# Last layer of a two-layer graph kernel: aggregate the packed binary features first, multiply by the signed weight afterwards

## The chip, the cores and the metric

The kernel runs on one core of a Trainium2 chip. The metric is the device time of one execution in microseconds, as the median of several runs. An execution has five engines that run their own instruction queues in order: PE (TensorE, matmuls and its weight loads), DVE (VectorE), ACT (ScalarE), POOL (GpSimd) and SP (SyncE, which here only starts DMAs). POOL also starts DMAs from its own queue. Engines wait for one another by semaphores.

## The reference, cut to what matters

There are N = 3327 nodes and D = 512 features. `adj` is a 3327 x 3327 matrix of zeros and ones, about 1% of them ones.

```python
# two attention layers (L0), then
x = layernorm(x + L0(x, adj, W_stack))
# the last layer:
bw  = sign(weight)                    # 512 x 512, values -1, 0, 1
ba  = max(sign(x), 0)                 # 3327 x 512, values 0, 1
out = relu(adj @ (ba @ bw.T))
x   = layernorm(x + out)
```

An attention layer is `proj = x @ W`, split into `Wh` and `Ws`, `a = softmax(Wh Ws^T) * adj`, `leaky_relu(a @ Wh + x)`.

## The kernel before, in words

Rows are cut into NT = 26 tiles of 128 (the last has 127). Two tiles make a half-chunk `g`, and NQ = 13 half-chunks of 256 columns cover the matrix. For each of the two attention layers `l` there is `project(l)`, which makes keys and values with a Strassen-like scheme of seven products in place of eight, and `attention(l)`, which walks over 169 steps `(g, q)`: query half-chunk `g` against key half-chunk `q`.

The order of all work is written out by hand. In step `v` of `attention`, a list `work` of pairs (place in the step between 0 and 1, closure) is sorted and issued; each engine's queue is then in that order. PE gets seven f32 products of step `v` for the aggregation (`values`, L834) and the scores of a step 30 half-steps ahead (`scores`, L588). DVE subtracts the column maximum (`shift`), adds the running total, multiplies by the adjacency (`masked`, L769) and ACT takes the exponential. POOL then makes four sums of that block (`sums`, L807 to L810), which PE reads two steps later.

Preparation of the last layer is strewn into the same steps:

- For half of the steps of each layer, the adjacency block of the step (`adj`, 128 x 512 f32, four buffers, loaded by SP) is turned into a Strassen set of seven fp8 blocks: `halved_sums` makes four sums on DVE (L789), `halved` copies the other three on ACT (L775, L776), `keep_blocks` stores the 112 KB to memory from POOL's queue (L792). `exact` (DVE, L798) counts entries that are neither 0 nor 1.
- When a half-chunk `g` of layer 1 is done, `finish(g)` returns a list of closures, one popped per step: `residual`, `sign` (moments of the row and the binary feature `ba`), `lay` and `turn` (store to memory, reload in another layout, transpose), `linear` (`ba @ bw`, four PE matmuls with 512 columns, L953), and a store of `xw`.
- `load_products` reloads `xw` and makes its Strassen sums on DVE (`product_sums`, L212 to L215).

After the last step comes a `fill`: PE runs products of the last layer while DVE ends `finish(12)`. Then `finale` runs over the 13 half-chunks. In half-chunk `g`, PE does 7 x 13 = 91 aggregation matmuls (`aggregate`, L1199: fp8 adjacency as the stationary operand, f16 features of 256 columns as the moving one). `take_out` combines the seven products on ACT and DVE. Per tile, `standard` (two ACT operations) normalizes `h`, `moments` (three DVE operations, then an ACT square root) adds the aggregate and takes mean and variance, and `scaled` (DVE reciprocal and scaling, then a store from POOL's queue) writes the output tile. `load_h(g + 1)` is issued by SP in the middle of half-chunk `g`; the tiles `ho` have four buffers, so the load of tile t waits until the store of tile t - 4 has landed. The places of the steps of the half-chunk before are

```python
(0.05, lambda: take_out(g - 1, 3)),
(0.12 if g == NQ - 1 else 0.08, lambda: scaled(u1, nc.gpsimd)),
(0.1, lambda: moments(u2, c_of[g - 1][1])),
(0.2, lambda: scaled(u2, nc.gpsimd)),
```

The last half-chunk is followed by a branch on the count of `exact`; the slow branch is not taken with these inputs.

Of the kernel before, what the change touches and what calls it, by code (L numbers as in the profile page):

```python
# [9 lines left out]
F32 = mybir.dt.float32  # L10
# [16 lines left out]
FAR = -1e30  # L27


@with_exitstack  # L30
def kernel(
# [51 lines left out]
    ident_h = keep.tile([P, P], BF16, name="ident_h")  # L83
    nc.vector.tensor_copy(ident_h, ident)
# [7 lines left out]

# [10 lines left out]
    ba_d = tc.dram_tile([NT, P, D], BF16, name="ba_d")  # L103
    xw_d = tc.dram_tile([NT, P, D], F16, name="xw_d")
    adj_d = tc.dram_tile([NQ, P, NQ, 7, P], F8, name="adj_d")
# [443 lines left out]
    def binary_weight(k, wt):  # L549
        neg = ring.tile([P, D], BF16, tag="xr", name=f"neg_w_{k}")  # L550
        nc.vector.tensor_scalar(neg, wt, 0.0, None, ALU.is_lt)
        sg = keep.tile([P, D], BF16, name=f"bw_{k}")
        nc.vector.scalar_tensor_tensor(sg, wt, 0.0, neg, ALU.is_gt, ALU.subtract)
        bw.append(sg)

    def attention(l, att):
# [215 lines left out]
        def halved(g, q):  # L772

            at, t = adj[g, q], adj[g, q, "b"]
            nc.scalar.copy(t[:, 0:2], at[:, :, :P], saturate=False)  # L775
            nc.scalar.copy(t[:, 2], at[:, 1, P:], saturate=False)  # L776

        def halved_sums(g, q):
            at = adj[g, q]
            t = adj[g, q, "b"] = att.tile(  # L780
                [P, 7, P], F8, tag="adj_b", bufs=3, name=f"ab_{l}_{g}_{q}"
            )
            a11, a21, a12, a22 = (at[:, k, ts(i, P)] for k in range(2) for i in range(2))
            s1, s2, s3, s4 = (t[:, i] for i in range(3, 7))
            for to, a, b, op in (
                (s1, a21, a22, ALU.add), (s2, s1, a11, ALU.subtract),
                (s3, a11, a21, ALU.subtract), (s4, a12, s2, ALU.subtract),
            ):
                nc.vector.tensor_tensor(to, a, b, op, saturate=False)  # L789
# [4 lines left out]
        def exact(g, q):  # L794

            at = adj.pop((g, q))
            i = g * NQ + q
            nc.vector.scalar_tensor_tensor(  # L798
                at, at, 0.0, at, ALU.is_gt, ALU.not_equal, accum_out=cnt[:, i : i + 1],
            )  # L800
# [72 lines left out]
        def finish(g):  # L873
# [37 lines left out]
            def sign(i):  # L911

                t, hh = mine[i], hs[i]
                r = rows(t)
                st = small.tile([P, 6], F32, tag="bn", name=f"bn_{t}")
                nc.vector.bn_stats(st[:r], hh[:r])
                nc.vector.bn_aggr(mv[:r, t, :], st[:r])
                ba = held[i] = att.tile([P, D], BF16, tag="ba", bufs=1, name=f"ba_{t}")
                nc.vector.tensor_scalar(ba[:r], hh[:r], mv[:r, t, 0:1], None, ALU.is_gt)
                if g < NQ - 2:  # L920
                    nc.gpsimd.dma_start(out=ba_d[t], in_=ba)

            def lay(i):

                bt = held[i] = ring.tile([P, P // B, P], BF16, tag="xr", name=f"bt_{mine[i]}")
                load_laid(nc.sync, bt, ba_d[mine[i]], P)

            def turn(i):

                r = rows(mine[i])  # L930
                if g < NQ - 2:
                    bt = held[i]
                    held[i] = att.tile([P, KD, P], BF16, tag="baT", bufs=1,
                                       name=f"baT_{mine[i]}")
                    nc.vector.transpose(
                        held[i].rearrange("p k (r v) -> p r k v", v=B),
                        bt.rearrange("p r (u k) -> p r k u", u=B),
                    )
                    return
                by_tile = held[i].rearrange("p (u k) -> p k u", k=KD)  # L940
                pt = ps_tr.tile([P, KD, P], BF16, tag="tr", name=f"pbt_{mine[i]}")
                for k in range(KD):
                    nc.tensor.transpose(pt[:, k, :r], by_tile[:r, k], ident_h[:r, :r])
                held[i] = att.tile([P, KD, P], BF16, tag="baT", bufs=1, name=f"baT_{mine[i]}")
                nc.scalar.copy(held[i][:, :, :r], pt[:, :, :r])

            def linear(i):

                t = mine[i]
                r = rows(t)  # L950
                pw = ps_tr.tile([P, D], F32, tag="tr", name=f"pxw_{t}")
                for k in range(KD):
                    nc.tensor.matmul(  # L953
                        pw[:r], held[i][:, k, :r], bw[k], start=(k == 0), stop=(k == KD - 1)
                    )
                if g >= NQ - 2:
                    nc.scalar.copy(xw[t][:r], pw[:r])
                    return
                xh = att.tile([P, D], F16, tag="ba", bufs=1, name=f"xwh_{t}")
                nc.scalar.copy(xh[:r], pw[:r])  # L960
                load_rows(nc.gpsimd, xw_d[t], xh, r)
# [5 lines left out]
            free = [] if g == NQ - 1 else [lambda: None]  # L967
            if g < NQ - 2:
                return [
                    norm, lambda: residual(0), lambda: sign(0), lambda: lay(0), lambda: None,  # L970
                    lambda: (turn(0), fetch(1)), lambda: linear(0), lambda: residual(1),
                    lambda: sign(1), lambda: lay(1), lambda: None, lambda: turn(1),
                    lambda: linear(1),
                ]
            return [
                *(free if g == NQ - 2 else []), norm, lambda: residual(0), lambda: (sign(0), fetch(1)), *free,
                lambda: turn(0), lambda: linear(0), lambda: residual(1), lambda: sign(1), *free,
                lambda: turn(1), lambda: linear(1),
            ]

        if last:
# [3 lines left out]
            def load_weight(k):  # L985
                wts[k] = ring.tile([P, D], F32, tag="h", name=f"wT_{k}")
                nc.sync.dma_start(out=wts[k], in_=weightT.rearrange("(p k) n -> k p n", k=KD)[k])
# [63 lines left out]
        first_products = NQ * NQ - EARLY  # L1051
        for v in range(-LOOK - 4, len(steps)):
# [25 lines left out]
            if v + 2 in blocks:  # L1078
                of = blocks[v + 2]
                work += [  # L1080
                    (0.6, lambda: halved_sums(*of)), (0.62, lambda: exact(*of)),
                    (0.61, lambda: halved(*of)),
# [9 lines left out]
            if last and 0 <= v - first_products < EARLY:  # L1092
                p = v - first_products
                work += [(0.5, lambda i=i: aggregate(0, 0, p, i)) for i in BANKS[0]]
# [4 lines left out]
            if last:  # L1099
                load_products(v, att)  # L1100
        if not last:
# [4 lines left out]
        fill = [  # L1106
            (g, b, p, i) for g, b in ((0, 1), (0, 2), (1, 0), (1, 1), (1, 2), (1, 3))
            for p in range(EARLY) for i in BANKS[b]
        ]
        for e, (n, do) in enumerate(zip((4, 16, 44, 8, 10, 12, 12, 8, 7), later)):  # L1110
            do()
            if e == 6:
                product_sums(EARLY)
# [6 lines left out]

    JL = 2
    NS = -(-NQ // JL)
    SOON = 5
    EARLY = NQ - 2
    XH = NT // 2
    BANKS = (0, 1), (2, 3), (4, 5), (6,)  # L1130
    BLOCKS = 0, 1, 4, 5, 3, 6, 2
    xw, xw_tiles, xt, ah, po = {}, [], {}, {}, {}

    def load_products(v, att):

        first = NQ * (NQ - 3), NQ * NQ - 16
        if v in first:
            xh = ops.tile([P, XH, D], F16, tag="gs", name=f"xw_{len(xw_tiles)}")  # L1140
            xw_tiles.append(xh)
            for a in range(XH):
                xw[len(xw)] = xh[:, a]
        if v == first[1] and rows(NT - 1) < P:
            nc.gpsimd.memset(xw[NT - 1], 0.0)
        for t in range(2 * NQ - 4):
            g, i = divmod(t, 2)
            made = (g + 1) * NQ - 1 + (7, 13)[i]
            if v == max(made + 3, first[t // XH] + t % XH):
                nc.sync.dma_start(out=xw[t], in_=xw_d[t])  # L1150
        p = v - NQ * (NQ - 1) - 2
        if SOON <= p < EARLY:
            product_sums(p)

        p, odd = divmod(v - first[0] - XH, 2)
        if 0 <= p < SOON and not odd:
            product_sums(p, att)
# [4 lines left out]
    def product_sums(p, att=None):  # L1162
        x1, x2 = xw[2 * p], xw[2 * p + 1]
        if p < SOON:
            tags = (("xs1",), ("xs1",), ("top1",), ("p1", "u2"), ("p5", "u3"))[p]
            n = 4 // len(tags)
            xt[p] = []
            for tag in tags:
                pool = ops if tag == "xs1" else att
                t = pool.tile([P, n, HD], F16, tag=tag, bufs=2 if tag == "xs1" else 1,  # L1170
                              name=f"xsum_{p}_{tag}")
                xt[p] += [t[:, i] for i in range(n)]
# [259 lines left out]
```

## Time and profile before

| | |
|---|---|
| median of 3 runs | 2595.97 us (2594.74 to 2597.7) |
| span of the profiled execution, first to last instruction | 2595.6 us |
| PE busy | 2568.4 us, 99% |
| DVE busy | 2105.2 us, 81% |
| POOL busy | 1095.6 us, 42% |
| ACT busy | 789.7 us, 30% |
| last product of `values` ends | about 2455.8 us |
| last product of `aggregate` starts | 2585.1 us |

The span of the profiled execution is its own time as far as the page tells it; what lies around the span is smaller than the spread of the runs, and the span stands 0.4 us under their median. Busy times are sums over instructions. A matmul's duration includes its passage through the array, so a stream of them is read by the distance of their starts and not by the duration.

### The profile page before, as it was taken

What the parts mean: (1) busy time and instruction counts of PE and PEld (TensorE: products, weight loads), DVE (VectorE), ACT (ScalarE), POOL (GpSimd) and SP (SyncE); (2) the same over time, 40 slices, a digit from 0 to 9 for tenths busy, and PEclk for the clock granted to TensorE, in tenths of its full rate; (3) what the DMA queues carried; (4) which work ended last, traced back from release to release, by engine and by line L of the source; (5) the groups of instructions that cost most, each with busy time, mean ns of one, the idle gap of its engine ahead of it and who ended that gap; (6) DMA issues with size and microseconds to landing.
All of it is one profiled execution on the core that took longest, in us unless ns stands there. A gap on an engine that the chain in (4) does not pass through costs nothing.

```text
span 2595.6 us, 40143 instructions
## 1 busy us (share of the span) xinstructions
PE 2568.4 (99%) x12423; PEld 2234.3 (86%) x12448; DVE 2105.2 (81%) x4444; ACT 789.7 (30%) x1956; POOL 1095.6 (42%) x1979
## 2 busy tenths in 40 slices
PE   9999999999999999999999999999999999999998
PEld 7888888888888888887888888888888888888787
DVE  5865988889898888768875778988889888878976
ACT  2323333323333333221332333333233333222243
POOL 2640343444444444456662144444444444455611
PEclk9999999999999999999999999999999999999999
DMA  6857777777777777687866877787777777777875
GB/s 206 294 202 228 241 251 231 262 238 257 255 236 259 241 239 239 229 263 254 299 242 198 249 251 251 251 268 247 257 258 253 262 248 248 245 260 261 291 252 186
DMA packets 330058, 642.63 MB, mean 248 GB/s; under 512 B 48957, under 2 KB 189621, under 8 KB 329582
## 3 DMA queue, kind: packets, MB, share of 16 engines
q1 hardware_dynamic: 293086, 530.89, 63.0%
q0 software_dynamic: 36752, 109.10, 11.2%
q8 instruction: 102, 1.67, 0.3%
q14 instruction: 118, 0.97, 0.1%
HBM read 530.29 MB, written 109.55 MB: 247 GB/s over the span
## 4 chain that ended last, share of the span: by engine, by line
PE 95%; DVE 3%; issue 1%; DMA 1%; ACT 0%; POOL 0%; SPq 0%; DVEq 0%; POOLq 0%; ACTq 0%
PE acc L834 37%; PE pZ L588 20%; PE pY L588 10%; PE pX L588 5%; PE agg L1199 5%; PE pZ_wh L408 4%; PE pD L588 3%; PE pZ_g L464 3%; PE pY_wh L408 2%; PE pY_g L464 2%; PE pm L312 1%; PE pX_wh L408 1%; PE pX_g L464 1%; PE pxw L953 1%; DVE s L753 1%
## 5 line engine op out<-in xcount | busy, mean ns | idle before, releaser
L588 PE MATMUL pZ<-gs,xs 128*128 128x256 f32 x2496 | 635.9, 379 | 0.9 <-ACT u L605 0.7
L588 PEld LDWEIGHTS pZ<-gs,xs 128*128 128x128 f32 x2496 | 473.8, 190 | 66.6 <-ACT u L605 1.1
L807 POOL TENSOR_TENSOR as<-s 128x128 f32<-128x128 f32 x338 | 163.9, 485 | 848.7 <-DVE s L769 656.9
L834 PE MATMUL acc<-ws,s 128*128 128x256 f32 x1352 | 402.1, 379 | 0.0
L834 PE MATMUL acc<-wh,s 128*128 128x256 f32 x1352 | 355.4, 379 | 0.0
L834 PE MATMUL acc<-ws,as 128*128 128x256 f32 x1352 | 347.6, 379 | 2.6 <-POOL as L809 2.6
L588 PE MATMUL pY<-gs,xs 128*128 128x256 f32 x1248 | 320.4, 379 | 0.0
L759 ACT ACTIVATE s<-s 128x512 f32<-128x512 f32 x338 | 213.4, 631 | 285.6 <-DVE s L753 284.3
L834 PEld LDWEIGHTS acc<-ws,as 128*128 128x128 f32 x1352 | 256.4, 190 | 42.9 <-POOL as L809 5.3
L834 PEld LDWEIGHTS acc<-wh,s 128*128 128x128 f32 x1352 | 256.9, 190 | 34.9
L834 PEld LDWEIGHTS acc<-ws,s 128*128 128x128 f32 x1352 | 256.0, 190 | 34.5
L588 PEld LDWEIGHTS pY<-gs,xs 128*128 128x128 f32 x1248 | 236.9, 190 | 32.6 <-ACT p L605 0.3
L658 DVE TENSOR_TENSOR top<-top,s 128x512 f32<-128x512 f32 x286 | 198.0, 707 | 75.2 <-ACT s L645 45.1
L753 DVE TENSOR_TENSOR s<-s,off 128x512 f32<-128x512 f32 x338 | 247.3, 732 | 0.5
L769 DVE TENSOR_TENSOR s<-s,adj 128x512 f32<-128x512 f32 x338 | 240.3, 711 | 8.1 <-DMA adj<-in_adjT_dram 2.4
L764 DVE TENSOR_TENSOR total<-total,s 128x512 f32<-128x512 f32 x312 | 231.4, 742 | 0.0
L605 ACT COPY u<-pZ 128x256 f32<-128x256 f32 x312 | 116.0, 372 | 354.9 <-PE pZ L588 352.9
L809 POOL TENSOR_TENSOR as<-s 128x128 f32<-128x128 f32 x338 | 199.3, 590 | 26.5
L808 POOL TENSOR_TENSOR s<-s 128x128 f32<-128x128 f32 x338 | 190.4, 563 | 27.3
L834 PE MATMUL acc<-wh,as 128*128 128x256 f32 x676 | 201.2, 379 | 0.0
L810 POOL TENSOR_TENSOR as<-s,as 128x128 f32<-128x128 f32 x338 | 179.0, 529 | 26.5
L630 DVE TENSOR_TENSOR s<-p,u 128x256 f32<-128x256 f32 x156 | 66.3, 425 | 142.6 <-ACT u L605 141.7
(239 smaller groups left out, 3880.3 us busy)
## 6 DMA issues: line engine op xcount, KB each, us to landing
ws<-ws_d SPq DMA_DIRECT2D x338, 512.0 KB
xs<-xs_d SPq DMA_DIRECT2D x182, 512.0 KB
adj<-in_adjT_dram SPq DMA_DIRECT2D x351, 256.0 KB
xs<-xs_d SPq DMA_DIRECT2D x156, 384.0 KB
gs_d<-gsp POOLq DMA_DIRECT2D x88, 256.0 KB, 3.1
gs<-gs_d SPq DMA_DIRECT2D x74, 256.0 KB
adj_d<-ab POOLq DMA_DIRECT2D x169, 112.0 KB, 4.2
ahl<-adj_d SPq DMA_DIRECT2D x78, 224.0 KB
```

What stands on the lines that cost most here:

```text
L408: nc.tensor.matmul(bank, of[LEFT[i]][:, k], wr[RIGHT[i]][:, k], start=(start and k == 0), stop=(k == 1), skip_group_check=True,)
L588: nc.tensor.matmul(ch[bank], xs[c, q, a][:, k], gs[c][:, b, k], start=(start and k == 0), stop=(k == 1), skip_group_check=True,)
L658: nc.vector.tensor_tensor(top[i], top[i], t, ALU.max)
L753: nc.vector.tensor_tensor(s, s, off[g].to_broadcast([P, 2, HW]), ALU.subtract)
L759: nc.scalar.activation(sc[g, q], sc[g, q], AF.Exp)
L764: nc.vector.tensor_tensor(total[g], total[g], sc[g, q], ALU.add)
L769: nc.vector.tensor_tensor(s, s, adj[g, q], ALU.mult)
L807: nc.gpsimd.tensor_tensor(s3, a11, a21, ALU.subtract)
L808: nc.gpsimd.tensor_tensor(a21, a21, a22, ALU.add)
L809: nc.gpsimd.tensor_tensor(s2, a21, a11, ALU.subtract)
L810: nc.gpsimd.tensor_tensor(s4, a12, s2, ALU.subtract)
L834: nc.tensor.matmul(acc[g][i // 2][:, i % 2], a[i], b[i], start=(q == 0 and i % 2 == 0), stop=(q == NQ - 1), skip_group_check=True,)
```

## The change

The product is taken in the other order, `(adj ba) bw^T`. The two halves of the 512 binary features are packed into one f16 number, low half plus 1024 times high half (`FIELD`), so that one matmul of the aggregation carries both. The adjacency is kept as plain fp8 blocks with no Strassen sums, and it becomes the moving operand; the packed features `pk` are the stationary one. A half-chunk has 13 x 2 x 2 = 52 aggregation matmuls of 256 columns in place of 91. The sum is split into its two fields in `split` (one ACT and two DVE operations), and `linear` runs in `finale`, per tile four matmuls of 512 columns. A field holds a node's degree at most, so that a check of the degrees is added: `degrees` sums the adjacency per partition on POOL, two additions of 128 x 256 per block, and `check` looks at the sums in the middle of `finale`.

```diff
+FIELD = 1024.0
+deg = keep.tile([P, NQ, HW], F8, name="deg")
-ba_d = tc.dram_tile([NT, P, D], BF16, name="ba_d")
-xw_d = tc.dram_tile([NT, P, D], F16, name="xw_d")
-adj_d = tc.dram_tile([NQ, P, NQ, 7, P], F8, name="adj_d")
+pk_d = tc.dram_tile([P, NT, HD], F16, name="pk_d")
+adj_d = tc.dram_tile([NQ, P, NQ, 2, HW], F8, name="adj_d")
...
-        def halved(g, q):
...
-        def halved_sums(g, q):
...
+        def narrow(g, q):
+            t = adj[g, q, "b"] = att.tile(
+                [P, 2, HW], F8, tag="adj_b", bufs=2, name=f"ab_{l}_{g}_{q}"
+            )
+            nc.scalar.copy(t, adj[g, q], saturate=False)
+
+        def degrees(g, q):
+            for a in range(2):
+                nc.gpsimd.tensor_tensor(deg[:, g], deg[:, g], adj[g, q][:, a], ALU.add, saturate=False)
...
-                at, at, 0.0, at, ALU.is_gt, ALU.not_equal, accum_out=cnt[:, i : i + 1],
+                dull, at, 0.0, at, ALU.is_gt, ALU.not_equal, accum_out=cnt[:, i : i + 1],
+                saturate=False,
...
-                ba = held[i] = att.tile([P, D], BF16, tag="ba", bufs=1, name=f"ba_{t}")
-                nc.vector.tensor_scalar(ba[:r], hh[:r], mv[:r, t, 0:1], None, ALU.is_gt)
-                if g < NQ - 2:
-                    nc.gpsimd.dma_start(out=ba_d[t], in_=ba)
-            def lay(i):
...
-            def turn(i):
...
-            def linear(i):
...
+                top_ = att.tile([P, HD], F16, tag="op1", bufs=1, name=f"ba_{t}")
+                nc.vector.tensor_scalar(
+                    top_[:r], hh[:r, HD:], mv[:r, t, 0:1], FIELD, ALU.is_gt, ALU.mult
+                )
+                if g < SOON:
+                    to = att.tile([P, HD], F16, tag="ou2", bufs=1, name=f"pk_{t}")
+                else:
+                    to = pk[0][:, t]
+                nc.vector.scalar_tensor_tensor(
+                    to[:r], hh[:r, :HD], mv[:r, t, 0:1], top_[:r], ALU.is_gt, ALU.add
+                )
+                if g < SOON:
+                    nc.gpsimd.dma_start(out=pk_d[:, t], in_=to)
...
-                    (0.6, lambda: halved_sums(*of)), (0.62, lambda: exact(*of)),
-                    (0.61, lambda: halved(*of)),
+                    (0.6, lambda: narrow(*of)), (0.61, lambda: degrees(*of)),
+                    (0.62, lambda: exact(*of)),
...
-        for e, (n, do) in enumerate(zip((4, 16, 44, 8, 10, 12, 12, 8, 7), later)):
+        fill = [(g, p, a, e) for g in range(3) for p in range(EARLY) for a in range(2) for e in range(2)]
+        for n, do in zip((6, 40, 40, 40, 18), later):
...
-    SOON = 5
-    EARLY = NQ - 2
+    SOON = NQ - 3
+    EARLY = NQ - 1
...
-    def product_sums(p, att=None):
...
+    def aggregate(g, p, a, e):
+        if (p, a, e) == (0, 0, 0):
+            po[g] = ps_ch.tile([P, 2, HW], F32, tag="ch", name=f"agg_{g}")
         nc.tensor.matmul(
-            po[g, 4 if own else b][:, i % 2], ah[g, p][:, BLOCKS[i]], of,
+            po[g][:, e], pk[0][:, 2 * p + a, ts(e, P)], ah[g, p][:, a],
+            start=(p, a, e) == (0, 0, 0), stop=(p, a) == (NQ - 1, 1), skip_group_check=True,
         )
...
-        def take_out(g, b):
...
+        def split(g, i=None):
...
+            nc.scalar.activation(c, v, AF.Identity, scale=1.0 / FIELD, bias=near)
+            nc.vector.tensor_scalar(hi, c, WHOLE, WHOLE, ALU.add, ALU.subtract)
+            nc.vector.scalar_tensor_tensor(lo, hi, -FIELD, v, ALU.mult, ALU.add)
+
+        def linear(t):
+            g, i = divmod(t, 2)
+            pw[t] = ps_acc.tile([P, D], F32, tag="acc", name=f"pxw_{t}")
+            for k in range(KD):
+                nc.tensor.matmul(
+                    pw[t], r_of[g][0][:, k // 2, k % 2, ts(i, P)], bw[k],
+                    start=(k == 0), stop=(k == KD - 1),
+                )
...
+            work += [(0.1, lambda: standard(t1)), (0.4, lambda: standard(t2))]
...
+                work.append((1.01, lambda: split(g)))
             if g > 0:
                 u1, u2 = half_tiles(g - 1)
                 work += [
-                    (0.05, lambda: take_out(g - 1, 3)),
-                    (0.12 if g == NQ - 1 else 0.08, lambda: scaled(u1, nc.gpsimd)),
-                    (0.1, lambda: moments(u2, c_of[g - 1][1])),
-                    (0.2, lambda: scaled(u2, nc.gpsimd)),
+                    (0.4, lambda: linear(u1)), (0.5, lambda: moments(u1, pw[u1])),
+                    (0.6, lambda: linear(u2)), (0.7, lambda: moments(u2, pw[u2])),
+                    (0.75, lambda: scaled(u1, nc.gpsimd)),
+                    (0.95, lambda: scaled(u2, nc.gpsimd)),
                 ]
...
-            take_out(g0, 0)
...
+            for i, t in enumerate((t1, t2)):
+                split(g0, i)
+                linear(t)
+            moments(t1, pw[t1])
+            moments(t2, pw[t2])
+            scaled(t1, nc.gpsimd)
```

`load_h(g + 1)` stays at its place 0.5, and `ho` keeps its four buffers.

## The prediction

> **What bounds the kernel now.** I read the page first: busy shares and the chain that ended last.
>
> ```profile
> PE 2568.4 (99%) x12423; PEld 2234.3 (86%) x12448; DVE 2105.2 (81%) x4444; ACT 789.7 (30%) x1956; POOL 1095.6 (42%) x1979
> PE 95%; DVE 3%; issue 1%; DMA 1%; ACT 0%; POOL 0%; SPq 0%; DVEq 0%; POOLq 0%; ACTq 0%
> ```
>
> PE is the bound over the whole span. Since a share is an average over stages, I then asked for stretches (columns: length, busy time of PE, PEld, DVE, ACT, POOL, granted clock, DMA share, GB/s).
>
> ```profile
> 1600.00:2200.00 600.00, 599.21 (x2773) 522.49 (x2788) 523.99 (x1106) 189.54 (x476) 256.85 (x492) 1.00 0.77 255
> 2470.00:2530.00 60.00, 60.00 (x547) 53.38 (x545) 46.43 (x118) 26.98 (x51) 6.54 (x12) 1.00 0.74 243
> 2580.00:2596.00 16.00, 5.40 (x50) 4.59 (x47) 8.03 (x22) 2.04 (x5) 1.60 (x3) 0.77 0.20 70
> ```
>
> PE is full in the attention of layer 1 and full in the last layer, until a tail. The third view is the chain in order of time; its last two long pieces are the last layer, 59.82 / 547 = 0.109 us for one aggregation matmul.
>
> ```profile
> 2470.88 59.82 PE agg L1199 x547
> 2530.82 53.18 PE agg L1199 x487
> ```
>
> The timeline gives the price of `linear`: its four matmuls start at 2450.81 and the next product at 2451.67, so 0.217 us each, 0.87 a tile (one record of the four is missing).
>
> ```profile
> 2450.81 1.03 PE L953 MATMUL pxw<-bw,baT 128*128 128x512 bf16 x3
> 2451.67 0.59 PE L834 MATMUL acc<-wh,as 128*128 128x256 f32 x2
> ```
>
> **PE work, removed and moved.** Aggregation falls from 13 x 91 = 1183 to 13 x 52 = 676 matmuls: 507 x 0.109 = 55 us. If PE stayed the bound, the time would fall by 55 us. `linear` keeps its 26 x 0.87 = 22.6 us, but moves out of the attention. So two accounts, cut at 2455.8 us, where the last f32 product ends.
>
> Before the cut go 24 of the 26 `linear` (24 x 0.87 = 20.9), eight transposes (0.4) and 22 aggregations of half-chunk 0 (2.4): 23.7 us, from a stretch where PE is full (599.21 of 600). Nothing replaces them there on PE.
>
> After the cut, before needs 2595.6 - 2455.8 = 139.8 us. After the change PE has 676 x 0.109 + 26 x 0.87 = 96 us of work there, 7.4 a half-chunk. But something else sets that pace.
>
> **The ring of `ho` buffers.** A load of tile t waits for the store of tile t - 4. Before, both stores of the last half-chunk come at 0.08 and 0.2 of a half-chunk; now at 0.75 and 0.95, because `linear`, `moments` and `scaled` come late. ACT's queue has both `standard` of half-chunk g + 1 ahead of the square roots that `scaled` of g needs. So a circle closes: store of t lands, `ho` of t + 4 loads, ACT standardizes two tiles, two square roots, DVE scales, next store. One turn is one half-chunk. The end of before shows every piece, with little other DMA traffic (tiles 20, 21, then 24, 25):
>
> ```profile
> 2568.34 0.54 POOL L116 DMA_DIRECT2D out_dram<-ho  x1 [4.35 <-DVE ho L1270]
> 2571.00 0.54 POOL L116 DMA_DIRECT2D out_dram<-ho  x1 [2.11 <-DVE ho L1270]
> 2574.13 0.72 ACT L1227 ACTIVATE ho<-ho,nmean 128x512 f32<-128x512 f32 x1 [1.04 <-DMA ho<-h_d]
> 2577.90 0.72 ACT L1227 ACTIVATE ho<-ho,nmean 127x512 f32<-127x512 f32 x1 [2.29 <-DMA ho<-h_d]
> 2578.65 0.72 ACT L1228 ACTIVATE ho<-ho,rstd 127x512 f32<-127x512 f32 x1
> 2579.28 0.46 ACT L1262 ACTIVATE rs<-mo,eps 128x1 f32<-128x1 f32 x2
> 2580.63 1.19 POOL L116 DMA_DIRECT2D out_dram<-ho  x2 [9.10 <-DVE rs L1269]
> ```
>
> From a store's issue to the standardizing of its successor: 2574.13 - 2568.34 = 5.8 us, and 6.9 for the next, whose load is in two pieces. Two operations of 0.72 per tile make 1.5 us until the second tile starts. From the second tile's start to the next store: 2580.63 - 2577.90 = 2.7. A turn is 5.8 + 1.5 + 2.7 = 10.0 us at the least traffic. Under heavy loads of `ahl` the first part was longer:
>
> ```profile
> 2503.95 0.54 POOL L116 DMA_DIRECT2D out_dram<-ho  x1 [4.35 <-DVE ho L1270]
> 2515.41 0.72 ACT L1227 ACTIVATE ho<-ho,nmean 128x512 f32<-128x512 f32 x1 [3.65 <-DMA ho<-h_d]
> ```
>
> That is 11.5 us, and a turn of 15.7. I take 10.2, near the quiet rows: a half-chunk now loads 13 x 64 KB = 832 KB of adjacency, against 6 x 224 + 112 = 1456 KB, and SP issues it behind the loads of `ho`, so it is through before the next store. PE's 7.4 us fits inside a turn with 2.8 us idle; so do DVE's: `split` 0.55 + 0.68 (rows L1270, L1256), two `moments` of 1.6, two `scaled` of 0.7, 5.8 in all.
>
> **The sum after the cut.** The fill is 144 matmuls and half-chunk 0 has four more: 148 x 0.109 + 0.2 for the transposes = 16.4 us. `finish(12)` hides in it: before, its last moments come 9.3 us after the cut, and the square root and two `standard` follow in 4. Then `split` on ACT and DVE, 0.72 + 0.55 + 0.68 and hand-overs: 18.5. `linear` 0.9, two `moments` 3.2, `scaled` 0.75, hand-over 0.4: first store at 23.8. From there 11 turns to the store of tile 22. The check of degrees, three DVE operations on up to 1024 elements and two reductions, some 4 us, falls into DVE's slack of one turn; I charge 0.9. Then the tail: second `scaled` 0.4, a half `split` 0.8, `linear` 0.9, two `moments` 3.2, `scaled` and the last tile's constants 1.2, two ACT operations 1.5, and 6.3 from the last store's issue to the end (2589.3 to 2595.6 before): 14.4. Together 39.1 + 11 x 10.2 = 151.3 us, 11.5 more than before's 139.8.
>
> Span: 2595.6 - 23.7 + 11.5 = 2583.4. The median of the runs is 0.4 above the span, so 2584 us. Each 0.1 us of a turn is worth 1.1 us.
>
> **What is hidden.** `halved_sums` leaves DVE: 111.8 + 76.6 + 84.7 = 273 us of L789 in the attention, `turn`, `product_sums` some 35 more. DVE is off PE's path there, so nothing is gained directly. `narrow` on ACT is one copy of 512 (0.63, as L759) for two of 0.40 and 0.30. `sign` gains one DVE operation, about 0.2 a tile, beside PE. SP loses the `lay` and `xw` loads, POOL 44 stores, and gets 20 of `pk`; `keep_blocks` grows by an eighth. None has a place on the chain.
>
> `degrees` adds 338 POOL additions of 128x256. The trace has no fp8 one. Nearest is the f32 one of `finish`; the longest row is 1.72 us for 512 elements (L209).
>
> ```profile
> L876 POOL TENSOR_TENSOR total<-total 128x256 f32<-128x256 f32 x26 | 19.9, 764 | 0.3
> POOL as L807 <- DVE s L769: 656.9, 236, 9.5
> ```
>
> I take 0.76, so 258 us; at 1.72 it is 581. Both fit in the 656.9 us that POOL idles for DVE's `masked`. Queued behind a pair of additions are the next step's `sums`, which PE reads two steps (some 14 us) after, and the `keep_blocks` store. A pair costs 1.5 to 3.4 us of a step of 7, so PE should not wait; I charge nothing, and up to 25 us if that cover fails. Below nothing: PE waited 2.6 us for `as` in all, so no more can be gained. Beside a POOL addition a DVE operation of two inputs takes 0.94 in place of 0.69 (L769 at 2403.93 and 2402.72): 338 x 0.25 = 85 us against 273 taken off, so DVE still gets looser.
>
> A rule speaks against this move. The Trainium skill, GPSIMD Engine Reference, section Engine selection, sends elementwise additions to VectorE, GpSimd being about twice as slow; SBUF — State Buffer says that the port pair the two share is locked and that the loser waits fully. By that rule DVE would lose up to 338 x 0.76 = 257 us in place of 85, which nearly eats the 273, and the time would still be 2584.
>
> PE's clock is at 1.00 where it is full and 0.77 in the last stretch, where it is mostly idle. With 2.8 us idle a turn I leave it at 1.00 in the sum. The Trainium skill, TensorE: Matmul & The Clock Gate, Part 1, has the clock halve after an idle window of about 3.4 us. Half-chunks 1 and 2 have few matmuls and idle longer; by that rule their eight `linear` matmuls take 1.7 us more, which the ring hides.
>
> **The rivals.** (1) The ring does not pace: stores and loads take less than the rows say, or the order lets `ho` in earlier. Then PE does, at 7.4 us a half-chunk: 39.1 + 11 x 7.4 = 120.5, and 2595.6 - 23.7 - 19.3 = 2552.6. For it: PE is all the chain today. Against: SP waited 63.7 us for `out_dram` stores before `ho` loads even with the early stores. (2) Slower than before: the ring turns slowly because stores and loads share the DMA engines with `ahl`. At the median landing of a store, 4.2 us, and a load of 4.0 (one issued at 2495.1 was used at 2499.1), a turn is 12.4: 39.1 + 136.4 = 175.5, and 2607.6. It decides from a turn of 11.3, where 39.1 + 11 T reaches 139.8 + 23.7. For it: DMA at 0.74 today. Against: a third fewer bytes per half-chunk. (3) `degrees` holds up `sums` and PE stalls in the attention: 25 us eat the 23.7, about 2608. Decided from a stall of 0.07 us a step. Against: POOL at 42%.
>
> **How the numbers follow.** Forecast (a turn of 9.3 to 11.0) 0.60, its own range 2573 to 2592; rival 1 in full or part (below 9.3) 0.11; rival 2 (above 11.0) 0.16; rival 3 0.13. Runs of this kernel spread by 0.1%, so 0.2%, 5.2 us, is what can be told from no change. Faster (below 2590.8): the forecast but for its end, and rival 1: 0.68. Same: 0.13, from turns of 10.9 to 11.8 and small stalls. Slower: 0.19, rivals 2 and 3. The range 2566 to 2606 leaves out rival 1 in full (below a turn of 8.6), the worst of 2 and 3.
>
> **What would show it.** Stores L117 in pairs some 10 us apart in the last layer; PE idle about 2.8 us a half-chunk, ended by `split`; ACT waiting for `ho`; the cut near 2432; POOL near 1350 us, DVE below 1950. Wrong if PE is full in `finale`, if stores are 11.3 us apart or more, or if PE waits for POOL's `as` by more than some 5 us in the attention.

## The result, and the profile after

The changed kernel takes 2575.6 us (median of 4 runs, 2574.68 to 2580.08) against 2596.84 for the kernel before in the same comparison: a ratio of 0.9925, interval 0.9911 to 0.9939. The change makes it 21 us faster. One run of all those told below, of the kernel with more `ho` tiles, took 2942.82 us at a granted clock of 0.85 and is left out of that kernel's ratio. The profiled execution of the changed kernel is the slowest of the four: time 2580.08, span 2578.3; the other spans are 2572.9 to 2574.1. What is read from its trace is summed against 2578.3, and the reader should keep those 4 us in mind.

The page: busy time of each engine, and the shares of the chain that ended last.

```profile
PE 2524.8 (98%) x11925; PEld 2187.1 (85%) x11925; DVE 2017.3 (78%) x3661; ACT 776.7 (30%) x1758; POOL 1459.6 (57%) x2295
PE 90%; issue 5%; DVE 3%; POOL 1%; DMA 1%; ACT 0%; SPq 0%; POOLq 0%; DVEq 0%; ACTq 0%
```

PE lost 44 us of busy time, but its share of the chain fell too, from 95% to 90%: some of the end of the kernel is no longer PE's. The stretches say where (columns as before: length, PE, PEld, DVE, ACT, POOL, granted clock, DMA share, GB/s).

```profile
1600.00:2200.00 600.00, 600.00 (x2790) 528.00 (x2789) 512.40 (x916) 183.88 (x415) 381.32 (x595) 1.00 0.74 246
2470.00:2530.00 60.00, 48.12 (x352) 35.34 (x351) 36.57 (x79) 22.95 (x42) 6.47 (x12) 0.91 0.58 187
2530.00:2580.00 50.00, 29.34 (x213) 20.52 (x211) 25.28 (x59) 17.20 (x33) 5.38 (x10) 0.84 0.34 115
```

In the attention PE is as full as before; POOL works 381 us of the 600 in place of 257. In the last layer PE, full before, is idle a fifth of the time, and its clock is 0.91. The waits of PE and ACT (total, times, longest) name what ends that idle time:

```profile
PE pxw L1152 <- DVE r L1146: 27.4, 10, 5.9
PE acc L830 <- POOL as L805: 3.0, 5, 1.4
ACT ho L1131 <- DMA ho<-h_d: 62.7, 12, 5.9
```

PE waits for `split` in the last layer, ACT waits in every half-chunk for the loads of `ho`, and POOL's sums hold PE up for 3.0 us in all, as before (2.6). The cut, the transposes after the last f32 product, on the timeline:

```profile
2431.06 0.38 PE L881 MATMUL pz<-ident,total 128*128 128x128 f32 x2
```

And POOL's stores of the output, in pairs, some of the twelve:

```profile
2454.93 1.35 POOL L117 DMA_DIRECT2D out_dram<-ho  x2 [14.52 <-DVE rs L1173]
2464.59 0.54 POOL L117 DMA_DIRECT2D out_dram<-ho  x1 [8.31 <-DVE rs L1173]
2467.85 0.54 POOL L117 DMA_DIRECT2D out_dram<-ho  x1 [2.72 <-issue]
2478.04 1.18 POOL L117 DMA_DIRECT2D out_dram<-ho  x2 [9.65 <-DVE rs L1173]
...
2544.96 1.19 POOL L117 DMA_DIRECT2D out_dram<-ho  x2 [7.94 <-DVE rs L1173]
2554.24 1.20 POOL L117 DMA_DIRECT2D out_dram<-ho  x2 [8.09 <-DVE rs L1173]
2563.43 1.20 POOL L117 DMA_DIRECT2D out_dram<-ho  x2 [8.00 <-DVE rs L1173]
```

Eleven turns from 2454.93 to 2563.43 are 108.5 us, 9.86 each. The chain of waits in order of time shows one whole turn (start, length, what; pieces under 0.5 us, and those put down to "issue", left out), and it is the circle of stores and loads, with PE nowhere in it:

```profile
2544.96 2.31 DMA out_dram<-ho
2547.32 2.72 DMA ho<-h_d
2550.14 0.73 ACT ho L1131
2551.52 0.71 ACT ho L1131
2552.26 0.72 ACT ho L1132
2553.40 0.55 DVE ho L1174
```

The store lands after 2.31 us, the load of the tile four further takes 2.72, ACT standardizes two tiles, DVE scales, and the next store leaves at 2554.24. In the turns before this one the chain puts nearly the whole time between two pairs of stores (7.9 to 9.6 us) down to "issue", so it names no cause there; that is most of the 5% above. That the circle paces them too is read from ACT's waits, one in each half-chunk, and from the kernels with the ring opened.

### The profile page after: what moved, and what is told of

Read it like the earlier page. It is cut to its first block, busy times and chain, and to the rows that moved or that the text cites. A ratio compares the mean times of both kernels' runs of the same rounds, so it can differ in the third digit from the quotient of the medians.

```text
span 2578.3 us, 38264 instructions
## 1 busy us (share of the span) xinstructions
PE 2524.8 (98%) x11925; PEld 2187.1 (85%) x11925; DVE 2017.3 (78%) x3661; ACT 776.7 (30%) x1758; POOL 1459.6 (57%) x2295
## 4 chain that ended last, share of the span: by engine, by line
PE 90%; issue 5%; DVE 3%; POOL 1%; DMA 1%; ACT 0%; SPq 0%; POOLq 0%; DVEq 0%; ACTq 0%
PE acc L830 37%; PE pZ L589 20%; PE pY L589 10%; PE pX L589 5%; PE pZ_wh L409 4%; PE pD L589 3%; PE pZ_g L465 3%; PE pY_wh L409 2%; PE pY_g L465 2%; PE pm L313 1%; PE pX_wh L409 1%; PE pX_g L465 1%; PE pg L443 1%; DVE s L754 0%; POOL out_dram L117 0%
## 5 line engine op out<-in xcount | busy, mean ns | idle before, releaser
L803 POOL TENSOR_TENSOR as<-s 128x128 f32<-128x128 f32 x338 | 165.0, 488 | 606.8 <-DVE s L770 453.3
L659 DVE TENSOR_TENSOR top<-top,s 128x512 f32<-128x512 f32 x286 | 250.8, 882 | 100.3 <-ACT s L641 50.9
L783 POOL TENSOR_TENSOR deg<-deg,adj 128x256 fp8e4<-128x256 fp8e4 x338 | 279.9, 828 | 57.5 <-DMA adj<-in_adjT_dram 42.9
L754 DVE TENSOR_TENSOR s<-s,off 128x512 f32<-128x512 f32 x338 | 296.6, 878 | 0.6
L765 DVE TENSOR_TENSOR total<-total,s 128x512 f32<-128x512 f32 x312 | 270.9, 868 | 0.0
L770 DVE TENSOR_TENSOR s<-s,adj 128x512 f32<-128x512 f32 x338 | 249.2, 737 | 5.7
L804 POOL TENSOR_TENSOR s<-s 128x128 f32<-128x128 f32 x338 | 234.3, 693 | 26.9
L805 POOL TENSOR_TENSOR as<-s 128x128 f32<-128x128 f32 x338 | 226.1, 669 | 26.5
L631 DVE TENSOR_TENSOR s<-p,u 128x256 f32<-128x256 f32 x156 | 78.5, 503 | 199.8 <-ACT u L606 199.1
L806 POOL TENSOR_TENSOR as<-s,as 128x128 f32<-128x128 f32 x338 | 203.6, 602 | 26.5
```

Of the source, the lines that this page charges most:

```text
L659: nc.vector.tensor_tensor(top[i], top[i], t, ALU.max)
L754: nc.vector.tensor_tensor(s, s, off[g].to_broadcast([P, 2, HW]), ALU.subtract)
L765: nc.vector.tensor_tensor(total[g], total[g], sc[g, q], ALU.add)
L770: nc.vector.tensor_tensor(s, s, adj[g, q], ALU.mult)
L783: nc.gpsimd.tensor_tensor(deg[:, g], deg[:, g], adj[g, q][:, a], ALU.add, saturate=False)
L804: nc.gpsimd.tensor_tensor(a21, a21, a22, ALU.add)
```

## The experiments

Ten runs followed. The theory: before the cut PE paces, so its removed matmuls come off the time; after the cut the ring of four `ho` buffers paces, so that what PE is spared there is not seen; the degree sums are hidden. The rivals: PE or the loads of adjacency pace the last layer, and the degree sums reach PE.

**The changed kernel again**, in the same comparison as the two runs with more `ho` tiles and the one that standardizes in one operation.

> The changed kernel once more, for a second profile. The profiled execution of the first was 4 us slower than the other runs and had one turn of 13.4 us among turns of 9.2 to 10.3. If that turn is chance, this profile has a span near 2574, eleven turns of 9.3 to 9.5 us on average between the stores of the last layer, and the cut between attention and last layer again near 2431. If it belongs to the program, a turn of some 13 us is there again at the same half-chunk (3 to 4).

2576.24 us, ratio 0.9922 (0.9907 to 0.9938). Its eleven turns are 106.7 us, 9.70 each, more than the 9.3 to 9.5 that were expected if the long turn were chance. The one long turn, 12.2 us, is at the same place as above, so it belongs to the program.

**More `ho` tiles, in the changed kernel.**

```diff
-h = h_of[t] = att.tile([P, D], F32, tag="adj", bufs=4, name=f"ho_{t}")
+h = h_of[t] = slot([P, D], F32, f"ho_{t}")
```

> The changed kernel with the tiles ho taken from the large ring s (33 slots) in place of the four adj buffers, so that a load of ho waits for no store. Theory (the circle store, load, standardize, scale, store sets the pace): the circle is cut, stores come at PE's pace of 7.4 us a half-chunk, 11 x (9.9 - 7.4) = 27 us less, some 2549 us; PE's clock near 1.00 in the last layer. Rival (the long DVE and ACT chain split, linear, moments, scaled, or a slower PE clock sets the pace): stores stay 9 to 10 us apart and the time stays within 5 us of 2576.

2558.2 us, ratio 0.9853 (0.9835 to 0.9871): 18 us faster than the changed kernel (20 by the median of the three runs that the ratio rests on, 2556.24). Its profiled execution has a span of 2553.9. POOL's stores:

```profile
2476.30 1.19 POOL L117 DMA_DIRECT2D out_dram<-ho  x2 [6.20 <-DVE rs L1173]
2483.70 1.20 POOL L117 DMA_DIRECT2D out_dram<-ho  x2 [6.21 <-DVE rs L1173]
2494.10 1.19 POOL L117 DMA_DIRECT2D out_dram<-ho  x2 [9.20 <-DVE rs L1173]
2503.09 1.19 POOL L117 DMA_DIRECT2D out_dram<-ho  x2 [7.80 <-DVE rs L1173]
2510.49 1.19 POOL L117 DMA_DIRECT2D out_dram<-ho  x2 [6.21 <-DVE rs L1173]
```

Nine of the eleven turns are now 7.2 to 7.6 us, most of them 7.39 to 7.41, which is PE's own work of a half-chunk (7.4). The ring was the pace, and loads of adjacency are not. The miss against the expected time, some 5 us in the profiled execution, is in the other two turns, 10.40 and 8.99: `check` puts 4.7 us on DVE there. With the ring closed, all but 0.9 us of that work fell into DVE's slack; in a turn of 7.4 us DVE has some 1.9 us to spare (by the 44.21 of 60 us in a stretch of the run with the early check, below).

**The same edit in the kernel before.** (The edit is that of the diff above.)

> The same edit on the kernel before the change. Theory: there PE is full in the last layer and the ring only fills gaps of ACT, so nothing changes, 2597 us within 3. Rival (the ho loads slow the last layer of either kernel): 5 to 25 us faster.

2597.01 us, ratio 1.0003 (0.9994 to 1.0012): nothing. The ring is a limit that the change brought out. It did two things that can have done so: it moved the stores from the start of a half-chunk to its end, and it cut PE's work of a half-chunk from 91 x 0.109 = 9.9 us, longer than a quiet turn of 9.4, to 7.4. No run parts the two.

**The reduction of degrees ahead of the half-chunks, with more `ho` tiles.**

```diff
         constants()
         load_h(0)
+        check()
...
-            if g == NQ // 2:
-                work.append((0.5, check))
```

> The changed kernel with the tiles ho in the large ring (as in the run with more ho tiles), and with the reduction of degrees and counts on VectorE issued ahead of the half-chunks, where VectorE sits idle for 7.4 us during the fill, in place of the middle of half-chunk 6. Theory (with the ring open PE paces the half-chunks at 7.4 us, and the only longer ones are the 10.4 and 9.0 us around that reduction, 4.6 us in all): eleven turns of 7.4 us, 81.4 in place of 86.0, and a time 4.6 us below that run, 2551 to 2553. Rival (the two long turns are from something else that falls there, such as loads of adjacency): they stay, and the time stays at 2556 to 2558.

2552.66 us, ratio 0.9827 (0.9813 to 0.984). The stretch of the last layer that stood at 48.12 of 60 us of PE and a clock of 0.91:

```profile
2470.00:2530.00 60.00, 59.89 (x487) 47.22 (x486) 44.21 (x102) 31.53 (x57) 8.67 (x16) 1.00 0.61 203
```

The two long turns are gone, PE is full, and the clock is 1.00. The first and the last pair of the twelve:

```profile
2456.22 1.35 POOL L117 DMA_DIRECT2D out_dram<-ho  x2 [14.52 <-DVE rs L1173]
2538.19 1.20 POOL L117 DMA_DIRECT2D out_dram<-ho  x2 [6.21 <-DVE rs L1173]
```

Eleven turns take 2538.19 - 2456.22 = 82.0 us, against 86.0 with the check in the middle; the intervals of the two ratios overlap, so what the earlier check is worth is read from these turns. This version beats both kernels: 44 us under the kernel before and 23 under the changed one.

**Standardizing in one operation, with the ring of four kept.**

```diff
-nc.scalar.activation(h, h, AF.Identity, bias=nmean[:r, t : t + 1])
-nc.scalar.activation(h, h, AF.Identity, scale=rstd[:r, t : t + 1])
+nc.scalar.activation(h, h, AF.Identity, scale=rstd[:r, t : t + 1], bias=nmean[:r, t : t + 1])
```

(and `nmean` multiplied by `rstd` once).

> The changed kernel with standard as one ACT operation (scale and bias together, bias multiplied by the scale beforehand) in place of two; the four buffers stay. Theory: two of the four ACT operations in the circle go, 2 x 0.75 = 1.5 us a turn, 11 x 1.5 = 16.5 us less, some 2559 us. Rival (the pace is set outside the circle): ACT has slack, and the time stays within 4 us of 2576.

2572.16 us, ratio 0.9911 (0.9896 to 0.9926): 4 us below the 2576.24 of the changed kernel in the same comparison, a quarter of what was expected. The four runs lie below those four, but the intervals overlap, and the time is within the 4 us that the rival named; that the pace is set inside the circle is shown by the open ring and not here. The turn of `check` is 10.31 as ever, since DVE sets it. Without it and the one after POOL's late store, the nine others fell from a mean of 9.42 to 8.68. One of them, between two pairs of stores, with ACT's two operations:

```profile
2530.08 1.19 POOL L117 DMA_DIRECT2D out_dram<-ho  x2 [7.13 <-DVE rs L1175]
2535.74 1.52 ACT L1132 ACTIVATE ho<-ho,nmean,rstd 128x512 f32<-128x512 f32 x2 [5.98 <-DMA ho<-h_d]
2538.51 1.20 POOL L117 DMA_DIRECT2D out_dram<-ho  x2 [7.25 <-DVE rs L1175]
```

ACT's piece, four operations and 2.84 us in most turns of the changed kernel, is two operations and 1.52 us here (1.5 to 1.8 in the last five turns). But the piece from the store to the first operation, 5.7 us here, is 5.5 in the mean of these five, 5.2 in the changed kernel. Elsewhere ACT stands waiting where it had worked. In the turn of `check`:

```profile
2499.00 0.81 ACT L1132 ACTIVATE ho<-ho,nmean,rstd 128x512 f32<-128x512 f32 x1 [5.34 <-DMA ho<-h_d]
2500.43 0.81 ACT L1132 ACTIVATE ho<-ho,nmean,rstd 128x512 f32<-128x512 f32 x1 [0.62 <-DMA ho<-h_d]
```

ACT is done with the first tile before the second has been loaded. And in two more turns the work of PE and DVE behind `split` comes out: from the end of ACT's standardizing to the next store it is 3.1 and 2.2 us in place of 1.26, in the first of them with the four matmuls of `linear` taking 1.9 us in place of 1.03. So what a piece of a circle is worth can be less than its length, where something that ran beside it comes out. Why the piece from the store to the first operation is longer, the runs do not show.

**The two edits together, standardizing in one operation and the early check with more `ho` tiles.**

> The changed kernel with the tiles ho in the large ring, the reduction of degrees ahead of the half-chunks, and the standardizing as one ScalarE operation. Theory (with the ring open PE paces the half-chunks, and ScalarE's operations lie beside it): what took 4 us off with the ring closed takes nothing off here; eleven turns of 7.4 us and a time within 2 us of the 2552.7 of the run with the early reduction alone. Rival (ScalarE's operations are on the path at any pace): another 4 us, about 2548.7.

2551.93 us, ratio 0.983 (0.9816 to 0.9844), against 2552.66: no difference that these runs can tell. Eleven turns again take 82.0 us. The same operations that were worth some 4 us inside the circle are worth nothing that shows beside a PE that paces.

**One store from another engine.** In every variant of the changed kernel so far, the second store of the second pair leaves 3.3 us after the first (2467.85 above, idle 2.72 for "issue"), where other pairs are 0.65 apart, and with the ring of four the turn around it is 12.2 to 13.5 us.

```diff
-(0.95, lambda: scaled(u2, nc.gpsimd)),
+(0.95, lambda: scaled(u2, nc.scalar if g == 2 else nc.gpsimd)),
```

> The changed kernel with one store moved: that of tile 3, which GpSimd issued 3.3 us after that of tile 2 where the other pairs are 0.65 us apart, is issued by ScalarE. Theory (it is the late issue on GpSimd, for which the trace shows no wait, that makes the turn after it 12 to 13 us, because tile 7 is loaded into the buffer that this store empties): tile 3 is stored within 1 us of tile 2, the turn falls to about 9.4 us, and the time by 2.5 to 3.5 us, to about 2573. Rival (something else at this place makes the turn long, such as the loads of adjacency ahead of it): the turn stays above 11.5 us and the time at 2576.

2578.55 us, ratio 0.9936 (0.9922 to 0.995): not faster. POOL's stores around the place:

```profile
2462.97 0.54 POOL L117 DMA_DIRECT2D out_dram<-ho  x1 [8.08 <-DVE rs L1173]
2476.05 1.07 POOL L117 DMA_DIRECT2D out_dram<-ho  x2 [12.54 <-DVE r L1146]
```

Tile 3 was stored at 2463.36 by ACT and its successor loaded in time, but the next pair left only at 2476.05, although DVE had scaled its tiles by 2473.8, and the turn stayed at 13.1. Time and turn are as the rival had it, so the theory that this store's lateness alone makes the turn long fell. The view puts POOL's wait down to `split` on DVE (L1146), which ended at 2475.12, 0.9 us before the store. That the same pause moved on to the next store, and so hangs on a place in POOL's order of instructions, is a reading and not shown. The loads of adjacency do not make the turn long by themselves: where the ring is open they run too, the same 2.72 us is in the trace, and the turn is 7.2. The run without the degree sums, below, has the pause as well. What POOL does in it stays open.

**Without the degree sums.**

```diff
-(0.6, lambda: narrow(*of)), (0.61, lambda: degrees(*of)),
+(0.6, lambda: narrow(*of)),
```

> The kernel after the change without its 338 GpSimd additions of degrees (the array of degrees keeps its first values). Theory (the additions stand beside other work, off PE's path): the time stays within 3 us of the changed kernel's 2576; GpSimd's busy time falls by the 280 us of the additions to about 1180, and VectorE's falls too, because its two-input operations no longer run beside them: L754 from a mean of 878 ns back to about 730, the whole engine from 2017 to about 1800. If the price that the prediction used for that (85 us) was right, VectorE falls only to about 1930. Rival (the additions hold up the sums that PE reads): the cut between attention and last layer comes up to 25 us earlier, and the time is near 2551.

2575.78 us, ratio 0.992 (0.9907 to 0.9934): the time is unchanged. In the profiled execution the cut lies at 2427.25, 3.8 us earlier than in the trace above, where the other variants of the changed kernel lie between 2429.7 and 2432.4; so up to some 3 us in the attention may be the sums' doing, and the medians do not show them. The busy times on its page, then one of DVE's groups (busy time, mean ns), first of the changed kernel and then of this one:

```profile
PE 2520.7 (98%) x11925; PEld 2186.0 (85%) x11925; DVE 1878.4 (73%) x3661; ACT 770.4 (30%) x1758; POOL 1166.8 (45%) x1957
```

```profile
L754 DVE TENSOR_TENSOR s<-s,off 128x512 f32<-128x512 f32 x338 | 296.6, 878 | 0.6
```

```profile
L754 DVE TENSOR_TENSOR s<-s,off 128x512 f32<-128x512 f32 x338 | 256.1, 758 | 0.6
```

DVE is relieved of 2017.3 - 1878.4 = 139 us, although none of the 338 additions ran on it: 0.41 us of delay on DVE for each addition of 0.83 us on POOL. The theory had expected 220.

**The degree sums on VectorE.**

```diff
-nc.gpsimd.tensor_tensor(deg[:, g], deg[:, g], adj[g, q][:, a], ALU.add, saturate=False)
+nc.vector.tensor_tensor(deg[:, g], deg[:, g], adj[g, q][:, a], ALU.add, saturate=False)
```

> The changed kernel with the 338 additions of degrees on VectorE in place of GpSimd. Theory (VectorE has slack in the attention, and its pairing with GpSimd costs as much as the additions themselves): 338 operations of 256 elements at 0.42 to 0.45 us, the row of the other 256-element additions, are 142 to 152 us more on VectorE, while its two-input operations fall back by some 220 us; so VectorE is busy less than in the changed kernel, about 1950 us against 2017, and the time stays within 3 us of 2576. Rival (VectorE is near its limit and every operation added to it is late for PE): VectorE over 2100 us busy, PE waits for it in the attention, and the time is 10 us or more above 2576.

2578.23 us, ratio 0.9931 (0.9918 to 0.9945): 2 us above the changed kernel, within what these runs can tell. The additions in the groups of this run:

```profile
L783 DVE TENSOR_TENSOR deg<-deg,adj 128x256 fp8e4<-128x256 fp8e4 x338 | 177.1, 524 | 5.9
```

They take 0.52 us, more than the 0.42 to 0.45 expected from the f32 rows, and DVE ends at 2035.5 us and not at 1950: the expectation that this placement relieves DVE fell. Doing the sums costs DVE 157 us over the kernel without them, letting POOL do them costs it 139, and neither shows in the time.

**A quarter of `linear`, in the kernel before.**

```diff
+few = 1 if g < NQ - 2 else KD
-for k in range(KD):
+for k in range(few):
...
-        start=(k == 0), stop=(k == KD - 1)
+        start=(k == 0), stop=(k == few - 1)
```

> The kernel before the change, with one of the four matmuls of each linear in the attention of the last layer (22 tiles of the first eleven half-chunks; the values of these tiles are then partial sums). Theory (PE is full there, so every matmul taken away comes off the time): 66 matmuls of 0.217 us are 14.3 us, the time is about 2582 against 2596, and the cut falls from 2455.8 to about 2441.5. Rival (another engine sets the pace there, and PE only looks full): less than 3 us.

2584.88 us, ratio 0.9953 (0.994 to 0.9967), 11.8 us off; the interval holds the 14.3. The cut:

```profile
2441.54 0.38 PE L885 MATMUL pz<-ident,total 128*128 128x128 f32 x2
```

That is 14.3 us earlier than 2455.8, what the sum says (to the tenth is luck: the cut of the changed kernel lies 0.8 us apart in two profiles). PE work in the attention is worth its full time, as far as these runs can tell.

## Why the prediction was right, point by point

The forecast was 2584 us and the time is 2575.6: right in sign and mechanism, 8 us too high. Its own sum, term by term, against the profiled execution:

| term | predicted | trace |
|---|---|---|
| cut between attention and last layer | 2432 | 2431.06 |
| cut to first store | 23.8 | 23.9 |
| eleven turns | 112.2 | 108.5 |
| tail, with 0.9 for the check | 15.3 | 14.9 |
| end of the span | 2583.4 | 2578.3 |

The turns are the mis-sized term, 3.7 of the 5.1 us (in the second profile they are 106.7, 5.5 less than predicted); the cut gives 1.0. The way from the span to the median was put at 0.4 us. It is 1.8 from the span to the time of that execution and then 4.5 down to the median, since the slowest execution was profiled; with the 5.1 of the terms that makes up the 8 us. Two slips of the prediction weigh nothing: the pieces of its tail add up to 14.3 and not 14.4, and the stored blocks grow from 112 to 128 KB, a seventh and not an eighth.

**The cut.** PE was full in the attention, and the shortened `linear` showed that what is taken from PE there comes off the time: 24.7 us here. This is the whole of the gain: after the cut the changed kernel needs 147.2 us against 139.8.

**The ring.** It paces, as forecast, and the wider ring shows it with 18 us. A turn was put together as 5.8 + 1.5 + 2.7 from the rows of before, 10.0, and taken as 10.2. The turn in the chain above has 2550.14 - 2544.96 = 5.2, 2551.52 - 2550.14 = 1.4, and 2554.24 - 2551.52 = 2.7: 9.3. The last two pieces were right; the first, store to standardizing, was 0.6 us too long, and the 0.2 put on top for traffic is not there in the quiet turns. Two turns hide in the mean: the one with `check`, 10.3, which is 0.9 above the quiet ones as charged, and the one with POOL's pause, 13.45, for which the sum had no term; so the mean came closer to 10.2 than the quiet turns did, and that is luck. Without these two, the nine others are 9.4.

**Rival 1**, PE's pace, was wrong for this kernel and right as a price: it gave 120.5 us after the cut and 2552.6 in all. The kernel with the open ring and the early check needs 2552.5 - 2432.35 = 120.2 after its cut, and its time is 2552.66 (that the two times agree to the tenth is luck, with runs 4 us apart). **Rival 2**, a turn of 12.4 under the loads of adjacency, did not come: the mean turn is 9.86, and opening the ring brings 7.40 with the same loads. **Rival 3**, a stall by the degree sums, did not come: 3.0 us of waits for POOL's `as` against 2.6, and the same time without the sums.

**The price of the degree sums** was mis-sized, without a part in the time. POOL's additions were 0.83 us and not 0.76:

```profile
L783 POOL TENSOR_TENSOR deg<-deg,adj 128x256 fp8e4<-128x256 fp8e4 x338 | 279.9, 828 | 57.5 <-DMA adj<-in_adjT_dram 42.9
```

POOL stands at 1460 us and not 1350, also because its own four sums rose from 733 to 829 us; without the degree sums they are still 818, so that part is not theirs. DVE stands at 2017 and not below 1950. One part of the miss is the delay by POOL, 139 us and not 85. The other, larger part is not theirs: without the degree sums DVE still stands at 1878, some 80 above the 1797 that the prediction's 273 and 35 us leave of 2105. Some of its operations with two inputs are longer there than in the kernel before (the running maximum `top`, 759 ns against 707); why, stays open. By the rule of the Trainium skill (SBUF — State Buffer, Who interferes with whom: one of the two holds the port pair for a whole instruction and the other waits fully) an estimate from POOL's measured time would be up to 280. The measured 139 is half of it, so here the rule bounds the loss; how much of the additions ran beside operations with two inputs was not measured. On the other rule of the skill, that such additions belong on VectorE and are about twice as slow on GpSimd (GPSIMD Engine Reference, Engine selection), the runs show 0.83 against 0.52, and that the choice did not matter here.

**The clock** was left at 1.00. It was 0.91 and 0.84 in the two stretches above. Three of the groups of `linear` after an idle time on PE:

```profile
2466.20 1.04 PE L1152 MATMUL pxw<-bw,r 128*128 128x512 f16 x4 [3.00 <-DVE r L1146]
2479.65 1.89 PE L1152 MATMUL pxw<-bw,r 128*128 128x512 f16 x4 [5.87 <-DVE r L1146]
2509.18 1.89 PE L1152 MATMUL pxw<-bw,r 128*128 128x512 f16 x4 [2.72 <-DVE r L1146]
```

The four matmuls after an idle time of 5.87 took 1.89 us in place of 1.03, and also after one of 2.72. The Trainium skill (TensorE: Matmul & The Clock Gate, Part 1) names an idle window of about 3.4 us, free-running; the 2.72 shows that a shorter idle time can be followed by slow matmuls too, and after one of 3.00 they took 1.04, so the length of the idle time alone does not decide. It cost little, as the sum had it: in the turn from 2478.04 to 2487.92, with slow matmuls from 2479.65 on, the next store came 1.9 us after ACT's standardizing in place of 1.26; in the turn with the group at 2509.18 it came at 1.26, since PE had slack in the circle.

## What to carry to other kernels

When an edit moves a store later in a pipeline stage, or makes the stage shorter, ask which buffer that store empties, and add up the circle from that store through the reload to the next store: if the circle is longer than the stage's work, removed work buys nothing there. A reuse ring that costs nothing in one order of work (no change in the kernel before) can be the bound in another (18 us here), and only opening it shows what the next bound is, here 4.7 us of DVE that had been hidden. Take the gain from the stage where the engine is full, and price a piece of a circle only after asking what ran beside it.

## What the runs showed of the hardware that was not expected

GpSimd paused for 2.72 us between the same two stores in every variant of the changed kernel that issues both from it, with no wait in the trace; with the second of them on ScalarE, its next store left 2.2 us after both tiles were scaled. An fp8 addition of 128 x 256 on VectorE took 0.52 us, in the mean, longer than the f32 ones of as many elements in the same run (0.40 to 0.49). And 280 us of GpSimd work cost VectorE 139 us that appear on no line of their own, only as longer means.
